# Second attention layer: six more source tiles as two float32r parts, with their 0/1 matrices cast on GpSimd

## The chip, the core and the metric

The kernel runs on one core of a Trainium2 chip, in one launch. Engines are called by the profile's names: PE is TensorE's matmul, PEld its weight load, DVE is VectorE, ACT is ScalarE, POOL is GpSimd, SP is the engine that issues most DMAs. The metric is device time in microseconds (us), the median of the runs shown. Before the change it is 3557.16 us, with runs of 3549.43, 3557.16 and 3558.97.

## The reference

Four graph layers follow each other on x (3327 nodes, 512 features) with one adjacency matrix. Each adds its result to x after a layer norm and a relu. Layers 0 to 2 are attention layers with 8, 4 and 8 heads, layer 3 averages neighbours. The change is in layer 1, the second one:

```python
def _L1_gnn_ref(H, A, W, a_l, a_r):
    mask = A + jnp.eye(n, dtype=A.dtype) > 0
    Wh = (H @ W).reshape(n, N_HEADS, D_K)              # 4 heads of 128
    sl = jnp.einsum('nhd,hd->nh', Wh, a_l)
    sr = jnp.einsum('nhd,hd->nh', Wh, a_r)
    e = jax.nn.leaky_relu(sl[:, :, None] + sr.T[None, :, :], negative_slope=NEG_SLOPE)
    e = jnp.where(mask[:, None, :], e, -jnp.inf)
    alpha = jnp.nan_to_num(jax.nn.softmax(e, axis=2), nan=0.0)
    out = jnp.einsum('nhm,mhd->nhd', alpha, Wh).reshape(n, OUT_DIM)
    return jax.nn.elu(out)
```

## The kernel before, in words

Nodes are cut into 26 tiles of 128. Query tiles are worked on in seven chunks, six of four tiles and a last one of two. Source tiles lie in five groups, `JG`: three of six tiles (g0, g1, g2) and two of four (g3, g4).

The exponential of a leaky relu of a sum splits into a product of a query factor and a source factor, one such product (a = 0) where the sum is positive and another (a = 1) where it is not. So a head needs two matrix products: a 0/1 matrix that says which edges lie on the positive side, times a table of source rows scaled by the first factor; and the matrix of the remaining edges, times a table scaled by the second. Each table has 128 features and one column for the softmax's denominator, 129 columns in all.

For one head of one chunk, `attention` does this in layer 1. `matrices` makes the 0/1 matrices: a compare for each source tile (L670 on ACT, or L667 on DVE for tiles 18 to 25), then an AND with the mask (L674, DVE). They are fp8, in tiles called `tht`. After the products of a = 0 an exclusive or with the mask (L794, DVE) turns the same tile into the matrix of a = 1. The products run in passes: a pass is two query tiles against all 26 source tiles, so 52 matmuls, and a full chunk has 4 heads x 2 products x 2 passes = 16 passes. The layer has 104 passes, eight of them in the last chunk. A pass ends with two reductions on DVE that add the parts and leave PSUM (L780).

The table rows are float32 and are kept to float32's precision in one of two ways, by the group's letter in `KIND = "bssvv"`:

- "b" (g0): three bf16 pieces side by side, 387 columns. The fp8 matrix is the stationary operand as it is (L762).
- "s" (g1, g2) and "v" (g3, g4): two float32r parts, 258 columns (L759). The matrix is first copied to float32r by `real` (L639): on ACT into `ts` (three buffers) for "s", on DVE into `tv` (two buffers) for "v". One copy serves one pass.

The tables are loaded from HBM by SP for each head and each a (L714), one DMA a group, into a ring of seven equal buffers `ab`. They are written in the layer before by `pieces` (three bf16 pieces, with subtractions on POOL) or by `parts` (a copy on ACT and a subtraction on DVE).

Work for the next layer is strewn between the passes by `hooks.run`: for each finished query tile an elu and an add (L866 to L869, the add on POOL), a layer norm (the small POOL steps L350 to L352), a projection on PE (L413), the scaling of its tables (L450, DVE) and their three pieces (L387 on DVE, L391 and L397 on ACT, L395 on POOL).

Tiles come from pools with a fixed number of buffers, and a planner writes the final order of each engine's instructions, ahead of the program's order where buffers allow it. On the engine the order is then fixed: an instruction that waits holds up all behind it on that engine.

Of the kernel before, what the change touches and what calls it, by code (L numbers as in the profile page):

```python
# [25 lines left out]
F32 = mybir.dt.float32  # L26
BF16 = mybir.dt.bfloat16
# [10 lines left out]
P = 128  # L38
# [7 lines left out]
GP_ON_DVE = [(5, 12, 19), tuple(range(18, 26)), (4, 9, 14, 19, 24)]  # L46


KIND = "bssvv"


@with_exitstack
def tile_gnn(ctx: ExitStack, tc: tile.TileContext, x, adj, W0, a01, W1, al, ar, W2, a2,
# [60 lines left out]
    for l in range(3):  # L114
        H, DA, AO, HW = dims(l)
        if l == 1:
            abd.append([dram.tile([H, 2, P, nj, AO], BF16, name=f"ab{l}_{g}") if KIND[g] == "b" else
                        dram.tile([H, 2, P, nj, 2 * DA], F32, name=f"ab{l}_{g}") for g, (_, nj) in enumerate(JG)])
        else:
            abd.append([dram.tile([H, P, nj, HW], BF16, name=f"ab{l}_{g}") for g, (_, nj) in enumerate(JG)])  # L120
    y1d = [dram.tile([n * P, D], F32, name=f"y1_{c}") for c, (_, n) in enumerate(chunks)]
# [247 lines left out]
    def pieces(L, t, AB, pool, first, behind=None):  # L369

        l = L.l
        g, jj = jwhere[t]
        H, DA, AO, HW = dims(l)

        o, two = (t % 2, 2) if first else (0, 1)
        if o == 0:
            L.pt = pool.tile([P, H, 2, two, AO] if l == 1 else [P, H, two, HW], BF16, name="pt", bufs=3 if first else 2)
        pt = L.pt
        nc.gpsimd.memset(pt[:, :, :, o, 3 * DA:AO] if l == 1 else
                         pt[:, :, o].rearrange("p h (a w) -> p h a w", a=2)[..., 3 * DA:AO], 1.0)  # L380

        def dst(s, a):
            if l == 1:
                return pt[:, :, a, o, s * DA:(s + 1) * DA]
            return pt[:, :, o, a * AO + s * DA:a * AO + (s + 1) * DA]
        r = pool.tile([P, 2, H, DA], F32, name="r", bufs=2 if first else 1)
        sb = nc.vector.tensor_sub(r, AB, high(AB))  # L387
        if behind:
            after(sb, behind)
        for a in range(2):  # L390
            cp = nc.scalar.copy(dst(0, a), high(AB[:, a]))  # L391
            if behind:
                after(cp, behind)
        for a in range(2):
            nc.gpsimd.tensor_sub(dst(2, a), r[:, a], high(r[:, a]))  # L395
# [3 lines left out]
        if o == two - 1 and l == 1:  # L399
            for a in range(2):  # L400
                L.to_store.append((abd[l][g][:, a, :, js, :].rearrange("h p j w -> p h j w"), pt[:, :, a]))
        elif first and o == two - 1:
# [52 lines left out]
    def parts(L, t, AB, pool, first, behind=None):  # L455
# [2 lines left out]
        g, jj = jwhere[t]  # L458
        H, DA, AO, HW = dims(l)
        H2 = H // 2  # L460
        if l == 1 and KIND[g] != "b":
            for f in range(2):
                hs = slice(f * H2, (f + 1) * H2)
                pt = pool.tile([P, H2, 2, 2, DA], F32R, name="pt", bufs=2)
                v = pt.rearrange("p h a s d -> p s a h d")
                cp = nc.scalar.copy(v[:, 0], AB[:, :, hs])
                if behind:
                    after(cp, behind)
                nc.vector.tensor_sub(v[:, 1], AB[:, :, hs], v[:, 0].bitcast(F32))
# [164 lines left out]
    def real(a, g, ks, th):  # L634

        nj = JG[g][1]
        k0, k1 = ks[0], ks[-1] + 1
        t = mp.tile([P, 2, nj, P], F32R, name="ts" if KIND[g] == "s" else "tv", bufs=3 if KIND[g] == "s" else 2)
        (nc.scalar.copy if KIND[g] == "s" else nc.vector.tensor_copy)(t[:, :k1 - k0, :nj], th[a][g][:, k0:k1])  # L639
        return t  # L640

    ahead = {}
# [42 lines left out]
    def attention(L, hooks, open_next, close):  # L685
# [5 lines left out]
        for c, (t0, nt) in enumerate(chunks):  # L691
# [3 lines left out]
            for h in range(H):  # L695
# [47 lines left out]
                for a in range(2 if l == 1 else 1):  # L743
# [5 lines left out]
                    for ks, js in passes:  # L749
                        thr = {}  # L750
                        for j in js:
                            g, jj = jwhere[j]
                            if l == 1 and KIND[g] != "b" and g not in thr:
                                thr[g] = real(a, g, ks, th)
                            for k in ks:
                                if j == 0:
                                    acc[k] = accs.tile([P, 512], F32, name="acc")
                                if g in thr:
                                    mm = nc.tensor.matmul(acc[k][:, :2 * DA], thr[g][:, k - ks[0], jj, :], ab[a][g][:, jj, :],  # L759
                                                     start=(j == 0), stop=(j == NT - 1), skip_group_check=True)  # L760
                                elif l == 1:
                                    mm = nc.tensor.matmul(acc[k][:, :3 * DA], th[a][g][:, k, jj, :], ab[a][g][:, jj, :3 * DA],  # L762
                                                     start=(j == 0), stop=(j == NT - 1), skip_group_check=True)
                                else:
                                    o = 1 if deg else 0
# [11 lines left out]
                            continue  # L777
                        for k in ks:
                            if l == 1:
                                nc.vector.tensor_reduce(R[:, k, a, :], acc[k][:, :3 * DA].rearrange("p (s d) -> p d s", s=3),  # L780
                                                        AX.X, ALU.add)
                            else:
                                v = acc[k][:, :2 * AO].rearrange("p (a w) -> p a w", a=2)[:, :, :3 * DA]
# [114 lines left out]
    with tc.tile_pool(name="first", bufs=1) as fp:  # L898
# [47 lines left out]
        while hooks.small:  # L946
# [1 line left out]
    A, R = [("A", D, F32, n) for n in A_BUFS], ("R", PER * 2 * 129, F32, 1)  # L948
    ab, gt, tht = ("ab", JM * 400, BF16, 7), ("gt", PER * JM * P, FP8, 7), ("tht", PER * JM * P, FP8, 7)
    tags = [[A[0], ("R", PER * 2 * 65, F32, 1), tht, ("tr", JM * P, BF16, 5), ("abx", 4 * 400, BF16, 4), gt],  # L950
            [A[1], ("ab", JM * 258, F32R, 7), R, ("ts", 2 * JM * P, F32R, 3), ("tv", 2 * 4 * P, F32R, 2), tht[:3] + (10,)],
            [A[2], ab, ("R", PER * 2 * 65, F32, 1), tht, gt]]
    hooks.masks = in_steps([mask_steps(ip, t, g) for t, g in order[20:]])
    for l in range(3):
# [530 lines left out]
```

## Time and profile before

| what | value |
| --- | --- |
| median of three runs | 3557.16 us |
| the profiled execution's span | 3551.1 us |
| PE, PEld busy | 3442.3 us (97%), 3107.2 us (88%) |
| DVE, ACT, POOL busy | 2624.3 us (74%), 2507.0 us (71%), 618.8 us (17%) |
| layer 1's passes | from 1233 to 2072 us of the span |
| in there: PE, DVE, ACT, POOL busy | 822.8, 729.3, 705.4, 205.5 of 839 us |
| in there: DMA | 78% of the DMA engines' time, 279 GB/s |

The page gives no time for the profiled execution beside its span. The span lies between the fastest and the slowest of the three runs.

Busy time of an engine is the union of its instructions' spans. A row of the order of time gives start, duration, engine, line, operation and tiles, and in brackets how long the engine had idled before and what ended that. A row by shape gives the count, the busy time, the mean duration of one, and the idle time before. In a row of windows each engine has its busy time and its number of instructions, then come the granted clock of PE, the DMA share and GB/s.

### The profile page before, as it was taken

What the parts mean: (1) busy time and instruction counts of PE and PEld (TensorE: products, weight loads), DVE (VectorE), ACT (ScalarE), POOL (GpSimd) and SP (SyncE); (2) the same over time, 40 slices, a digit from 0 to 9 for tenths busy, and PEclk for the clock granted to TensorE, in tenths of its full rate; (3) what the DMA queues carried; (4) which work ended last, traced back from release to release, by engine and by line L of the source; (5) the groups of instructions that cost most, each with busy time, mean ns of one, the idle gap of its engine ahead of it and who ended that gap; (6) DMA issues with size and microseconds to landing.
All of it is one profiled execution on the core that took longest, in us unless ns stands there. A gap on an engine that the chain in (4) does not pass through costs nothing. (4 is left out here: it accounts for less than half of the span.)

```text
span 3551.1 us, 77646 instructions
## 1 busy us (share of the span) xinstructions
PE 3442.3 (97%) x30751; PEld 3107.2 (88%) x30751; DVE 2624.3 (74%) x5227; ACT 2507.0 (71%) x4113; POOL 618.8 (17%) x858
## 2 busy tenths in 40 slices
PE   7899999999999999999999989999999999999998
PEld 6789999999999888888888869989898989876887
DVE  7788888888887699888888868867676768672121
ACT  5777787878787789888888677767666757572111
POOL 6611222112111202222223320101010101020000
PEclk9999999999999999999999999999999999999999
DMA  7699999999857787777777875555545555576331
GB/s 207 223 282 251 233 263 238 268 260 250 256 203 247 246 285 276 279 269 273 269 273 254 332 268 190 191 175 189 183 166 181 185 172 188 168 271 257 105 107 54
DMA packets 398120, 797.72 MB, mean 225 GB/s; under 512 B 112970, under 2 KB 221845, under 8 KB 397105
## 3 DMA queue, kind: packets, MB, share of 16 engines
q1 hardware_dynamic: 363890, 723.14, 63.4%
q0 software_dynamic: 28128, 62.42, 7.6%
q10 hardware_dynamic: 5726, 7.08, 0.6%
q8 instruction: 245, 4.01, 0.5%
q14 instruction: 131, 1.07, 0.1%
HBM read 663.59 MB, written 129.64 MB: 223 GB/s over the span
## 5 line engine op out<-in xcount | busy, mean ns | idle before, releaser
L670 ACT ACTIVATE gt<-s1b,ks 128x512 fp8e4<-128x512 f32 (+1 forms) x2448 | 1448.2, 677 | 276.4 <-issue 160.1
L766 PE MATMUL acc<-ab,tht 128*128 128x195 bf16 (+1 forms) x9112 | 1553.1, 248 | 5.4 <-DVE tht L674 4.6
L769 PE MATMUL acc<-ab,gt 128*128 128x195 bf16 (+1 forms) x9112 | 1552.2, 248 | 5.0 <-DVE rc L806 3.3
L769 PEld LDWEIGHTS <-gt 128*128 128x128 fp8e4 x10744 | 1053.6, 98 | 40.1 <-issue 27.4
L766 PEld LDWEIGHTS <-tht 128*128 128x128 fp8e4 x10744 | 1053.4, 98 | 24.8 <-DVE tht L674 11.5
L674 DVE TENSOR_TENSOR tht<-gt,m 128x768 uint32<-128x768 uint32 (+3 forms) x557 | 445.5, 800 | 129.4 <-ACT gt L670 125.5
L676 DVE TENSOR_TENSOR gt<-tht,m 128x768 uint32<-128x768 uint32 (+3 forms) x557 | 448.0, 805 | 8.7
L639 ACT CAST ts<-tht 128x1536 fp32r<-128x1536 fp8e4 x208 | 300.0, 1470 | 55.6 <-PE acc L759 52.5
L759 PE MATMUL acc<-ab,ts 128*128 128x258 f32 x2496 | 333.4, 289 | 4.7 <-ACT ts L639 3.4
L759 PEld LDWEIGHTS acc<-ab,ts 128*128 128x128 f32 x2496 | 313.2, 190 | 13.2 <-ACT ts L639 3.8
L667 DVE TENSOR_SCALAR gt<-s1b,ns 128x512 fp8e4<-128x512 f32 (+1 forms) x446 | 218.2, 495 | 129.4 <-PE acc L769 125.1
L1021 PE MATMUL acc<-y,mf 128*128 128x512 f32 x1352 | 309.8, 391 | 1.1 <-DVE mf L1016 1.1
L670 ACT ACTIVATE tht<-s1b,ks 128x512 fp8e4<-128x512 f32 (+1 forms) x504 | 308.4, 680 | 2.3 <-DMA s1b<-s 1.7
L1021 PEld LDWEIGHTS acc<-y,mf 128*128 128x128 f32 x1352 | 253.6, 188 | 57.2 <-DVE mf L1016 1.5
L769 PE MATMUL acc<-abx,gt 128*128 128x195 bf16 (+1 forms) x1632 | 287.4, 249 | 11.6 <-DVE rc L806 5.6
L766 PE MATMUL acc<-abx,tht 128*128 128x195 bf16 (+1 forms) x1632 | 287.8, 249 | 4.6 <-DVE tht L674 3.0
L869 POOL TENSOR_TENSOR xt<-xt,e 128x512 f32<-128x512 f32 x72 | 121.9, 1693 | 916.8 <-DVE e L868 583.9
L784 DVE TENSOR_REDUCE R<-acc 128x130 f32<-128x390 f32 x416 | 214.2, 554 | 79.5 <-PE acc L769 78.9
L762 PE MATMUL acc<-ab,tht 128*128 128x387 bf16 x1248 | 225.8, 329 | 8.9 <-DMA ab<-ab 5.8
L1018 ACT CAST mf<-m 128x768 fp32r<-128x768 fp8e4 (+1 forms) x78 | 59.1, 762 | 244.5 <-PE acc L1021 232.7
L759 PE MATMUL acc<-ab,tv 128*128 128x258 f32 x1664 | 218.8, 283 | 1.4 <-DVE tv L639 1.2
L759 PEld LDWEIGHTS acc<-ab,tv 128*128 128x128 f32 x1664 | 207.2, 189 | 2.9 <-DVE tv L639 2.1
(163 smaller groups left out, 3710.2 us busy)
## 6 DMA issues: line engine op xcount, KB each, us to landing
ab<-ab SPq DMA_DIRECT2D x333, 600.0 KB, 5.3
ab<-ab SPq DMA_DIRECT2D x112, 774.0 KB, 6.5
ab<-ab SPq DMA_DIRECT2D x112, 516.0 KB, 5.3
ab<-ab SPq DMA_DIRECT2D x112, 400.0 KB, 4.0
abx<-ab SPq DMA_DIRECT2D x110, 400.0 KB, 7.9
ab<-ab SPq DMA_DIRECT2D x56, 582.0 KB, 7.3
s1b<-s SPq DMA_DIRECT2D x120, 256.0 KB, 6.5
m<-mask SPq DMA_DIRECT2D x69, 384.0 KB, 4.4
```

What stands on the lines that cost most here:

```text
L639: (nc.scalar.copy if KIND[g] == "s" else nc.vector.tensor_copy)(t[:, :k1 - k0, :nj], th[a][g][:, k0:k1])
L667: nc.vector.tensor_scalar(gv[:, :, jj, :], s1v, L.ns2[:, j, h:h + 1], 2.0, op0=ALU.is_gt, op1=ALU.mult, saturate=False)
L670: nc.scalar.activation(gv[:, :, jj, :], s1v, AF.Relu, bias=L.ks2[:, j, h:h + 1], scale=BIG, saturate=False)
L674: nc.vector.tensor_tensor(pu, gu, mu, ALU.bitwise_and)
L676: nc.vector.tensor_tensor(gu, pu, mu, ALU.bitwise_xor)
L759: mm = nc.tensor.matmul(acc[k][:, :2 * DA], thr[g][:, k - ks[0], jj, :], ab[a][g][:, jj, :], start=(j == 0), stop=(j == NT - 1), skip_grou ...
L762: mm = nc.tensor.matmul(acc[k][:, :3 * DA], th[a][g][:, k, jj, :], ab[a][g][:, jj, :3 * DA], start=(j == 0), stop=(j == NT - 1), skip_grou ...
L766: nc.tensor.matmul(acc[k][:, :3 * DA + o], th[0][g][:, k, jj, :], ab[0][g][:, jj, :3 * DA + o], start=(j == 0), stop=False, skip_group_che ...
L769: mm = nc.tensor.matmul(acc[k][:, AO:AO + 3 * DA + o], th[1][g][:, k, jj, :], ab[0][g][:, jj, AO:AO + 3 * DA + o], start=False, stop=(j == ...
L784: nc.vector.tensor_reduce(R[:, k], v.rearrange("p a (s d) -> p a d s", s=3), AX.X, ALU.add)
L869: nc.gpsimd.tensor_add(xt, xt, e)
L1021: nc.tensor.matmul(acc[k], mf[:, jj, :], y2[g][:, jj, s, :], start=(j0 + jj == 0 and s == 0), stop=(j0 + jj == NT - 1 and s == 1))
```

## The change

`KIND` becomes "gssvv". g0 is now treated as g1 to g4 are: two float32r parts, 258 columns, one matmul form for the whole layer. Its 0/1 matrix is copied from fp8 to float32r on POOL, 128x1536 elements a pass, into a new tile `tg` with two buffers. The bf16 pieces of layer 1 disappear, with their storage in HBM. The reduction at the end of a pass reads 258 columns instead of 387. Buffers change: the ring of seven `ab` becomes a ring of four for the groups of six tiles and a ring of three for the groups of four, and `tht` has nine buffers instead of ten.

```diff
-KIND = "bssvv"
+KIND = "gssvv"
...
         if l == 1:
-            abd.append([dram.tile([H, 2, P, nj, AO], BF16, name=f"ab{l}_{g}") if KIND[g] == "b" else
-                        dram.tile([H, 2, P, nj, 2 * DA], F32, name=f"ab{l}_{g}") for g, (_, nj) in enumerate(JG)])
+            abd.append([dram.tile([H, 2, P, nj, 2 * DA], F32, name=f"ab{l}_{g}") for g, (_, nj) in enumerate(JG)])
...
-        if l == 1 and KIND[g] != "b":
+        if l == 1:
             for f in range(2):
...
-        t = mp.tile([P, 2, nj, P], F32R, name="ts" if KIND[g] == "s" else "tv", bufs=3 if KIND[g] == "s" else 2)
-        (nc.scalar.copy if KIND[g] == "s" else nc.vector.tensor_copy)(t[:, :k1 - k0, :nj], th[a][g][:, k0:k1])
+        copy = {"g": nc.gpsimd.tensor_copy, "s": nc.scalar.copy, "v": nc.vector.tensor_copy}[KIND[g]]
+        t = mp.tile([P, 2, nj, P], F32R, name="t" + KIND[g], bufs=3 if KIND[g] == "s" else 2)
+        copy(t[:, :k1 - k0, :nj], th[a][g][:, k0:k1])
...
-                            tl = mp.tile([P, JM * 2 * DA], F32R, name="ab", bufs=7)
-                            two = KIND[g] != "b"
-                            w = 2 * DA if two else AO
-                            v = (tl if two else tl.bitcast(BF16))[:, :nj * w].rearrange("p (j w) -> p j w", j=nj)
-                            ld = nc.sync.dma_start(v.bitcast(F32) if two else v, abd[l][g][h, a])
+                            v = mp.tile([P, nj, 2 * DA], F32R, name=f"ab{nj}", bufs=4 if nj == JM else 3)
+                            ld = nc.sync.dma_start(v.bitcast(F32), abd[l][g][h, a])
...
-                        pt = mp.tile([P, PER * JM * P], FP8, name="tht", bufs=10 if l == 1 else 7)
+                        pt = mp.tile([P, PER * JM * P], FP8, name="tht", bufs=9 if l == 1 else 7)
...
-                            if l == 1 and KIND[g] != "b" and g not in thr:
+                            if l == 1 and g not in thr:
                                 thr[g] = real(a, g, ks, th)
...
-                                elif l == 1:
-                                    mm = nc.tensor.matmul(acc[k][:, :3 * DA], th[a][g][:, k, jj, :], ab[a][g][:, jj, :3 * DA],
-                                                     start=(j == 0), stop=(j == NT - 1), skip_group_check=True)
...
-                                nc.vector.tensor_reduce(R[:, k, a, :], acc[k][:, :3 * DA].rearrange("p (s d) -> p d s", s=3),
+                                nc.vector.tensor_reduce(R[:, k, a, :], acc[k][:, :2 * DA].rearrange("p (s d) -> p d s", s=2),
                                                         AX.X, ALU.add)
```

More of the change, by code (lines that the diff above doesn't have):

```diff
@@ L376, in pieces @@
         if o == 0:
-            L.pt = pool.tile([P, H, 2, two, AO] if l == 1 else [P, H, two, HW], BF16, name="pt", bufs=3 if first else 2)
+            L.pt = pool.tile([P, H, two, HW], BF16, name="pt", bufs=3 if first else 2)
         pt = L.pt
-        nc.gpsimd.memset(pt[:, :, :, o, 3 * DA:AO] if l == 1 else
-                         pt[:, :, o].rearrange("p h (a w) -> p h a w", a=2)[..., 3 * DA:AO], 1.0)
+        nc.gpsimd.memset(pt[:, :, o].rearrange("p h (a w) -> p h a w", a=2)[..., 3 * DA:AO], 1.0)
         def dst(s, a):
-            if l == 1:
-                return pt[:, :, a, o, s * DA:(s + 1) * DA]
             return pt[:, :, o, a * AO + s * DA:a * AO + (s + 1) * DA]
@@ L398, in pieces @@
         js = slice(jj + 1 - two, jj + 1)
[L399 to L402, printed above, removed]
+        if first and o == two - 1:
             if g not in ahead:
@@ L950, in tile_gnn @@
     tags = [[A[0], ("R", PER * 2 * 65, F32, 1), tht, ("tr", JM * P, BF16, 5), ("abx", 4 * 400, BF16, 4), gt],
-            [A[1], ("ab", JM * 258, F32R, 7), R, ("ts", 2 * JM * P, F32R, 3), ("tv", 2 * 4 * P, F32R, 2), tht[:3] + (10,)],
+            [A[1], ("ab6", JM * 258, F32R, 4), ("ab4", 4 * 258, F32R, 3), R, ("ts", 2 * JM * P, F32R, 3),
+             ("tg", 2 * JM * P, F32R, 2), ("tv", 2 * 4 * P, F32R, 2), tht[:3] + (9,)],
             [A[2], ab, ("R", PER * 2 * 65, F32, 1), tht, gt]]
```

## The prediction

> **What bounds the kernel now.** I read the page's busy shares, then windows over layer 1, then the order of time inside a pass, then rows by shape, and last POOL's rows. The windows (us; PE, PEld, DVE, ACT, POOL busy; clock, DMA share, GB/s), the second and third one full chunk each:
>
> ```profile
> 1300.00:1400.00 100.00, 98.30 (x744) 86.59 (x743) 95.06 (x177) 84.82 (x104) 13.99 (x14) 1.00 0.77 283
> 1493.70:1618.90 125.20, 125.01 (x915) 109.99 (x914) 110.23 (x203) 108.80 (x146) 32.77 (x37) 1.00 0.78 273
> 1618.90:1744.20 125.30, 125.29 (x918) 110.34 (x918) 109.72 (x201) 108.85 (x146) 35.65 (x38) 1.00 0.78 274
> 2000.00:2072.00 72.00, 61.21 (x391) 51.66 (x392) 50.92 (x114) 42.70 (x74) 26.93 (x37) 0.95 0.92 346
> ```
>
> In a steady chunk PE never stops, at full clock; DVE and ACT are 88% and 87% busy. In the last chunk PE loses some 11 of 72 us, with the DMA engines at 92%. So PE's own work sets the time in six chunks of seven, and DVE is next in line. A pass in the order of time:
>
> ```profile
> 1600.57 2.15 PE L762 MATMUL acc<-ab,tht 128*128 128x387 bf16 x12
> 1602.42 3.19 PE L759 MATMUL acc<-ab,ts 128*128 128x258 f32 x24
> 1605.44 2.08 PE L759 MATMUL acc<-ab,tv 128*128 128x258 f32 x16
> 1607.36 2.15 PE L762 MATMUL acc<-ab,tht 128*128 128x387 bf16 x12
> ```
>
> The starts give 1.85 us for g0's 12 matmuls (154 ns each), 3.02 us for 24 in float32r (126 ns), 6.79 us for the pass.
>
> How POOL and DVE get on decides the rest. The rows of the order of time, first one in which POOL waits, then one in which DVE does:
>
> ```profile
> 1618.76 2.15 DVE L794 TENSOR_TENSOR tht<-tht,m 128x768 uint32<-128x768 uint32 x3
> 1618.92 4.59 POOL L869 TENSOR_TENSOR xt<-xt,e 128x512 f32<-128x512 f32 x1 [0.70 <-DVE e L868]
> 1620.84 0.94 DVE L674 TENSOR_TENSOR tht<-tht,m 128x768 uint32<-128x768 uint32 x1
> 1621.71 0.68 DVE L639 CAST tv<-tht 128x1024 fp32r<-128x1024 fp8e4 x1
> 1622.31 1.01 DVE L780 TENSOR_REDUCE R<-acc 128x129 f32<-128x387 f32 x2
> 1623.55 0.63 ACT L866 ACTIVATE e<-A 128x512 f32<-128x512 f32 x1 [4.22 <-POOL xt L869]
> ```
>
> ```profile
> 1608.63 2.51 POOL L395 TENSOR_TENSOR pt<-r 128x520 bf16<-128x520 f32 x2 [15.94 <-DVE r L387]
> 1610.15 2.08 DVE L802 TENSOR_TENSOR R<-R,cpm 128x1032 f32<-128x1032 f32 x1
> ```
>
> The add L869 takes 1.26 us alone and 4.59 here: it gets in only when DVE reaches L780, which reads PSUM. The multiply L802, 1.22 us alone (at 1795.51), takes 2.08 behind L395. DVE work from SBUF and POOL work exclude each other; only DVE's idle time and its PSUM readers are free for POOL.
>
> **The change, part by part.**
>
> PE. Per pass 12 matmuls go from 154 to 126 ns: 0.34 us, 5.4 us per full chunk (125.2 to 119.8), 32.6 us for the 96 passes of full chunks, 35.4 for all 104.
>
> DVE. L780 takes 550 ns for 387 columns. L804 shows the price of a column: 287 ns for 130 elements and 420 for 260, 1.02 ns each. 129 columns fewer are 0.13 us, 32 reductions a chunk give 4.3 us. DVE goes from 110.0 (mean of the two full chunks) to 105.7 before the casts.
>
> The cast on POOL: 104 times 128x1536, fp8 to float32r, one input. No row has it. POOL's one-input rows:
>
> ```profile
> 1.18 0.28 POOL masks.py:199 TENSOR_SCALAR_AFFINE_SELECT ident<-ident 128x128 f32<-128x128 f32 x1
> L283 POOL COPY m<-dg x26: 199/209/1183, 1107.4 to 1972.2; 128x32 uint32<-128x32 uint32 x26
> L350 POOL TENSOR_SCALAR mv<-mv x104: 216/422/1111, 5.1 to 3213.2; 128x1 f32<-128x1 f32 x104
> L395 POOL TENSOR_TENSOR pt<-r x116: 1043/1057/4064, 31.4 to 2105.0; 128x520 bf16<-128x520 f32 x104, 128x516 bf16<-128x516 f32 x12
> ```
>
> (In the last three, the least, median and greatest ns.) From 216 ns for one element to 284 for 128 is 0.5 ns an element, 1.0 us for the cast: the lower end. From the 32-element copy (199) to 284 is 0.88: 199 + 1504 x 0.88 = 1.5 us. Two-input rows give 2.0 (L395) to 2.46 (L869) ns an element: 3.1 to 3.8 us, the upper end. I take 1.5, from the two one-input rows nearest to it, and keep 1.0 to 3.8. [...]
>
> What a cast costs DVE. Per chunk DVE leaves POOL 15.2 idle + 16.3 (L780, half of its 32.6 in the two chunks) + 5.1 (L450) = 36.6 us. POOL now has 8 subtractions of 1.05 and 4 adds of 1.26 a chunk, 13.4 us; DVE's instructions of the two chunks, each against the lowest tenth of its shape, are 14.3 us longer, 7.1 a chunk: 53%. For 16 x 1.5 = 24 us that is 12.7. Laying one cast per pass into the first free stretch after its buffer is released, on DVE's order of time of four chunks, leaves 10.1 us blocked. DVE then has 105.7 + 10.1 to 12.7 = 115.8 to 118.4 of 119.8 us, 97 to 99%. [...]
>
> What PE loses at such a load: in 1300 to 1400 DVE was 95% busy and PE 98.3% (the row above), 1.7%. I take 2% of six chunks (719 us), 14 us; between 0 and the whole 32.6.
>
> What queues behind the cast on POOL: adds, norm steps, subtractions, and the stores that POOL issues. ACT already waited 4.22 us for an add; a cast in front adds up to 1.5 us to some of 24. This is in the 2%. The casts themselves are early in the built order: 88 of 104 can start 91 or more of the layer's matmuls before the first that needs them, 11 us, and the laying above never takes longer than 10.4. Two have no lead, at the layer's start and in the last head's first pass. At the first, PE waits for the cast too: 1.5 us (0 to 3). At the other PE already waited 3.4 us for ACT's copy in the same place: 1 us (0 to 3).
>
> Loads. g0 grows from 582 to 774 KB, 56 times; SP now issues g3's load ahead of g1's, since its ring is its own. In full chunks the rings tell more: release to use shrinks from 61 to 65 matmuls to 53 for three of five groups, 8.4 to 6.5 us, against 6.5 us median from issue to landing of a 774 KB load and 5.3 of a 516 KB one. So no cover is left. At 0 to 0.8 us in each of 48 table rows this is 0 to 38 us; I take it as hidden in the 14 us, because a pass that waits for DVE gives a load the same time. In the last chunk 8 x 192 KB more at 346 GB/s are 4.5 us, and its 2.7 us of saved matmuls are lost to the DMA: 2 us taken (-2.7 to 4.5).
>
> `tht` with nine buffers: the tenth matrix now waits for g0's release, which the last cast gives nearly a pass before the last matmul did. PE waits 2.7 us for such matrices in the layer now; I take 0, between -2.7 and as much again. In layer 0 six tiles lose POOL subtractions (2.4 us a tile), four ACT copies become two, and one DVE subtraction of 1.23 us becomes two of 0.69: 0.9 us more on DVE in all, hidden under PE, which the page shows at 9 tenths there; 0, at most 0.9.
>
> Sum: -32.6 + 14 + 1.5 + 1 + 2 = -14 us. The profiled span of 3551 becomes 3537; from the median 3557 it is 3543.
>
> **Rivals.**
>
> Slow cast (ends slower). A cast of 2.6 us, between the one- and two-input rows, laid in the same way blocks 26 us a chunk: DVE 131.7 against 125.2 before, 6.5 x 6 = +39 and the edges: 3600. It decides at about 2.2 us, where DVE reaches 125. At 3.1 us it is +80. [...] Against: affine select.
>
> Waits eat it. The cast has 1.5 us, but at 97 to 99% DVE is late often enough to use up all of PE's gain: 3557 (3547 to 3570). For it: in-order queues and two-deep rings. Against: DVE waited 55 us for `tv` buffers alone, so it runs ahead.
>
> Late loads. 0.5 us in 48 rows on top of the rest: 3543 + 24 = 3567. For it: no cover. Against: three loads a row are issued 12 matmuls apart and need not queue.
>
> All of it comes. DVE stays ahead as at 88%: 3557 - 35 + 5 = 3527.
>
> **How the numbers follow.** Chances: forecast 0.47, slow cast 0.23, waits eat it 0.16, late loads 0.07, all of it 0.07. 0.3% is 10.7 us, about what a measurement tells from no change. The forecast's own range, 3531 to 3553, lies for seven tenths below 3546: faster 0.33 + 0.07 + 0.01 = 0.41. Same: 0.12 of the forecast, 0.08 of the waits, 0.01: 0.21. Slower 0.38. The range goes from the whole gain, 3527, to a cast of 2.8 us, 3612.
>
> **What would show it.** L759 with `tg` at about 126 ns a matmul and a pass of 6.45 us. The cast's least duration 1.5 us, its mean above 2. DVE above 95% in a chunk, with L639, L667, L802 and L809 longer. A chunk of 121 to 123 us. Wrong, if the cast takes 2.2 us or more alone, if PE idles before `tg` matmuls in steady chunks, or if DMA ends PE's waits there.

## The result, and the profile after

The change makes the kernel slower. The kernel after takes 3602.47 us (median of four runs, 3599.09 to 3604.38), the kernel before beside it 3553.30 (3548.75 to 3558.97). The ratio is 1.0138, with a 95% interval of 1.0123 to 1.0152. The forecast was 3543 us, a gain of 14; the outcome is a loss of 49. It lies inside the range, on the other side of the time before.

The page of the kernel after begins with the busy shares of its span of 3597.3 us:

```profile
PE 3427.8 (95%) x30751; PEld 3163.8 (88%) x30751; DVE 2693.7 (75%) x5233; ACT 2500.6 (70%) x4101; POOL 781.9 (22%) x944
```

PE's work is down by 14.5 us, DVE's is up by 69 and POOL's by 163. Over the whole span no share looks alarming, so the stage has to be read. Its windows, with the columns of the prediction's windows (us; PE, PEld, DVE, ACT, POOL busy; clock, DMA share, GB/s), are cut where every 832nd matmul of the layer begins; 832 matmuls are one full chunk. The first row is the second chunk, the last row the short last one:

```profile
1360.70:1495.60 134.90, 123.19 (x912) 118.62 (x913) 127.81 (x212) 110.67 (x149) 58.09 (x50) 0.96 0.73 258
1495.60:1625.70 130.10, 119.39 (x915) 115.05 (x914) 124.73 (x204) 117.01 (x160) 61.49 (x53) 1.00 0.77 279
1625.70:1759.50 133.80, 121.29 (x916) 116.46 (x914) 125.99 (x203) 110.45 (x147) 57.21 (x53) 0.99 0.75 270
1759.50:1891.90 132.40, 122.28 (x916) 117.98 (x915) 123.24 (x201) 109.21 (x145) 61.15 (x53) 0.97 0.76 269
1891.90:2024.90 133.00, 123.20 (x915) 119.41 (x914) 121.31 (x211) 104.76 (x150) 57.04 (x51) 0.96 0.74 260
2024.90:2115.00 90.10, 75.82 (x501) 70.67 (x500) 70.04 (x143) 56.33 (x98) 46.69 (x48) 0.91 0.93 348
```

Where the clock is 1.00 PE's work of a chunk is 119.39 us: the cheaper matmuls did come, 119.8 was forecast. But a chunk takes 130 to 135 us where it took 125. PE now idles some 11 us in it, and DVE is busy for 121 to 128 us, longer than PE's work. Cut in the same way, the traces of before and after give:

| layer 1, us | before | after |
| --- | --- | --- |
| first chunk | 124.1 | 127.4 |
| mean of chunks 2 to 6 | 125.7 | 132.9 |
| last chunk | 86.6 | 90.2 |
| all passes | 839.1 | 881.9 |
| PE idle in them | 15.9 | 80.3 |

So 43 of the 46 us between the two spans lie in layer 1, and 36 of them in five steady chunks.

The cast itself, from the answer on tile `tg` (least, median and greatest ns, first and last start in us):

```profile
L633 POOL CAST tg<-tht x104: 1458/1481/5020, 1227.6 to 2098.2; 128x1536 fp32r<-128x1536 fp8e4 x104
```

1.46 us alone; 1.5 was forecast. What it does to DVE is seen in the rows by shape of the layer (count, busy us and mean ns, idle us before). First before, then after:

```profile
L639 DVE CAST tv<-tht 128x1024 fp32r<-128x1024 fp8e4 x208 | 145.9, 702 | 55.1 <-PE acc L759 55.1
L667 DVE TENSOR_SCALAR tht<-s1b,ns 128x512 fp8e4<-128x512 f32 x192 | 93.8, 536 | 0.9 <-PE acc L762 0.9
L674 DVE TENSOR_TENSOR tht<-tht,m 128x768 uint32<-128x768 uint32 x72 | 67.9, 950 | 7.0 <-ACT tht L670 6.9
```

```profile
L633 DVE CAST tv<-tht 128x1024 fp32r<-128x1024 fp8e4 x208 | 168.0, 810 | 24.2 <-PE acc L750 24.2
L661 DVE TENSOR_SCALAR tht<-s1b,ns 128x512 fp8e4<-128x512 f32 x192 | 127.1, 701 | 0.0
L668 DVE TENSOR_TENSOR tht<-tht,m 128x768 uint32<-128x768 uint32 x71 | 78.2, 1101 | 11.8 <-ACT tht L664 11.5
```

The same instructions on the same shapes are 108, 165 and 151 ns longer in the mean. The reductions L768, which read PSUM, are not: all 208 took 405 to 430 ns. DVE's slack is seen in the idle time before `tv`: it waited 55.1 us for PE to free these buffers, and now 24.2. To put one number on it I take, for every DVE instruction of the layer, its duration less the lowest tenth of its operation and shape, and call the sum DVE's lengthening. It is 7.5 us in a steady chunk before and 24.8 after: 17.3 more for 16 casts, 1.08 us for each cast of 1.48. (Against the kernel without the cast, below, it is 15.2 us, 0.95 for each.)

One such place in the order of time (start, duration; in brackets the idle time before):

```profile
1643.16 1.92 DVE L661 TENSOR_SCALAR tht<-s1b,ns 128x512 fp8e4<-128x512 f32 x1
1643.30 1.48 POOL L633 CAST tg<-tht 128x1536 fp32r<-128x1536 fp8e4 x1
1644.99 0.68 DVE L633 CAST tv<-tht 128x1024 fp32r<-128x1024 fp8e4 x1
1645.59 0.47 DVE L661 TENSOR_SCALAR tht<-s1b,ns 128x512 fp8e4<-128x512 f32 x1
1645.73 1.22 PE L750 MATMUL acc<-ab,tv 128*128 128x258 f32 x8
1647.26 0.67 DVE L633 CAST tv<-tht 128x1024 fp32r<-128x1024 fp8e4 x1
1647.99 1.23 PE L750 MATMUL acc<-ab,tv 128*128 128x258 f32 x8 [1.04 <-DVE tv L633]
```

The compare L661 takes 0.47 us when nothing stands in its way (1645.59) and 1.92 when the cast runs inside it (1643.16): the difference, 1.45 us, is nearly the whole cast of 1.48. The two `tv` casts behind it come late, and PE stands still for 1.04 us before the second. The waits of the stage, by engine, line and cause (us in total, times, longest):

```profile
POOL tg L633 <- PE acc L750: 167.0, 38, 12.9
PE acc L750 <- DVE tv L633: 29.1, 23, 2.9
PE acc L750 <- DMA ab<-ab: 25.0, 22, 3.4
ACT e L854 <- POOL xt L857: 23.0, 9, 6.1
PE acc L750 <- ACT ts L633: 8.6, 7, 2.9
```

In the kernel before, the waits for tables, for `tv` and for the add were:

```profile
PE acc L762 <- DMA ab<-ab: 5.8, 3, 3.0
PE acc L759 <- DMA ab<-ab: 1.2, 2, 1.0
PE acc L759 <- DVE tv L639: 1.2, 2, 0.7
ACT e L866 <- POOL xt L869: 25.2, 10, 5.2
```

PE waits for DVE's copies first, and nearly as long for tables from HBM. POOL itself waits 167 us for PE to free `tg`, so it isn't short of time. But its cast comes too late in places, for DVE and not for PE: the exclusive or L782 overwrites a matrix that the cast must have read, and waits for it.

```profile
DVE tht L782 <- POOL tg L633: 14.6, 7, 2.6
```

### The profile page after: what moved, and what is told of

Its sections match the earlier page's. It is cut to its first block, busy times and chain, and to the rows that moved or that the text cites. A ratio compares the mean times of both kernels' runs of the same rounds, so it can differ in the third digit from the quotient of the medians.

```text
span 3597.3 us, 77815 instructions
## 1 busy us (share of the span) xinstructions
PE 3427.8 (95%) x30751; PEld 3163.8 (88%) x30751; DVE 2693.7 (75%) x5233; ACT 2500.6 (70%) x4101; POOL 781.9 (22%) x944
## 5 line engine op out<-in xcount | busy, mean ns | idle before, releaser
L757 PEld LDWEIGHTS <-gt 128*128 128x128 fp8e4 x10744 | 1053.3, 98 | 35.3 <-issue 24.8
L661 DVE TENSOR_SCALAR gt<-s1b,ns 128x512 fp8e4<-128x512 f32 (+1 forms) x446 | 217.1, 492 | 137.5 <-PE acc L757 133.4
L664 ACT ACTIVATE tht<-s1b,ks 128x512 fp8e4<-128x512 f32 (+1 forms) x504 | 309.6, 679 | 10.4 <-DMA s1b<-s 10.1
L750 PE MATMUL acc<-ab,tv 128*128 128x258 f32 x1664 | 229.5, 288 | 35.3 <-DVE tv L633 29.1
L633 POOL CAST tg<-tht 128x1536 fp32r<-128x1536 fp8e4 x104 | 181.3, 1747 | 239.8 <-PE acc L750 167.0
```

What stands on the lines that cost most here:

```text
L633: copy(t[:, :k1 - k0, :nj], th[a][g][:, k0:k1])
L661: nc.vector.tensor_scalar(gv[:, :, jj, :], s1v, L.ns2[:, j, h:h + 1], 2.0, op0=ALU.is_gt, op1=ALU.mult, saturate=False)
L664: nc.scalar.activation(gv[:, :, jj, :], s1v, AF.Relu, bias=L.ks2[:, j, h:h + 1], scale=BIG, saturate=False)
L757: mm = nc.tensor.matmul(acc[k][:, AO:AO + 3 * DA + o], th[1][g][:, k, jj, :], ab[0][g][:, jj, AO:AO + 3 * DA + o], start=False, stop=(j == ...
```

## The experiments

Three theories stood against each other, and the recorded expectations use their letters. P: POOL's cast and DVE's work in SBUF exclude each other, DVE falls behind PE, and PE waits for `tv`. L: the loads are late, because g0's tables are larger and the ring of seven buffers became rings of four and three. Q: POOL's queue is the trouble, since adds and stores wait behind casts. Each median below stands beside runs of the kernel before on the same chip, whose median was 3553 to 3557 us. "The passes" are the time from layer 1's first matmul of the passes to the end of the last.

**No cast at all.** One constant tile of ones takes the place of g0's matrix. This leaves out g0's proper contribution to the products.

```diff
         copy = {"g": nc.gpsimd.tensor_copy, "s": nc.scalar.copy, "v": nc.vector.tensor_copy}[KIND[g]]
+        if KIND[g] == "g":
+            if not fixed:
+                fixed.append(mp.tile([P, 2, nj, P], F32R, name="tg", bufs=1))
+                nc.vector.memset(fixed[0].bitcast(F32), 1.0)
+            return fixed[0]
```

> The changed kernel with GpSimd's cast left out: the matmuls of the first six source tiles read one constant float32r matrix instead, so those tiles' contribution to the second layer is left out of the result in its proper form. Matmuls, loads, buffer rings and all other work stay. [...] Theory L (the smaller rings of four and three make the table loads late): the loads still come late, 3570 to 3595 us. [...]

3534.82 us, ratio 0.9938 (0.9920 to 0.9957). The cast costs 67.7 us, 0.65 for each. The spans of the two traces differ by 63 us: 51 of them lie in the layer's passes, which take 831.0 us here, and 8 ahead of the passes, where neither kernel casts. By P and by Q the loss had to go with the cast, by L not, so the time alone doesn't tell P from Q. Two chunks of this kernel, with the columns as above:

```profile
1477.30:1599.80 122.50, 118.62 (x916) 114.96 (x915) 111.50 (x205) 116.15 (x159) 33.63 (x37) 1.00 0.82 293
1599.80:1722.40 122.60, 119.15 (x915) 115.95 (x914) 110.79 (x207) 110.98 (x151) 30.10 (x37) 0.99 0.83 293
```

DVE falls from some 125 us a chunk to 111, and PE's waits for `tv` from 29.1 us to under 1. What is left of PE's waits is L:

```profile
PE acc L756 <- DMA ab<-ab: 26.5, 24, 4.4
```

**No cast, and one ring of seven for all tables.** The same constant tile, and:

```diff
-                            v = mp.tile([P, nj, 2 * DA], F32R, name=f"ab{nj}", bufs=4 if nj == JM else 3)
+                            tl = mp.tile([P, JM * 2 * DA], F32R, name="ab", bufs=7)
+                            v = tl[:, :nj * 2 * DA].rearrange("p (j w) -> p j w", j=nj)
```

> As the kernel without the cast (the same part is left out), and the rings of four and three table buffers are one ring of seven again. Theory P: within 5 us of the kernel without the cast. Theory L: 15 to 40 us less than that one, and PE's waits for table loads, 25 us in the changed kernel's second layer, fall below 10 us.

3521.15 us, ratio 0.9903 (0.9882 to 0.9924): 13.7 us less than with the split rings; the passes alone take 808.9 us, 22 less. Neither expectation is met: P had at most 5 us, L at least 15 and waits below 10. PE's waits for tables are halved:

```profile
PE acc L757 <- DMA ab<-ab: 12.7, 11, 5.2
```

So L is real and worth 14 us where nothing else holds PE up, a fifth of the cast's price (22 of 51 in the passes alone). This kernel also shows that PE's gain is there for the taking: 33 us below the 3553.89 of before beside it, where 35.4 us of matmul time go.

**The cast made twice.**

```diff
         copy(t[:, :k1 - k0, :nj], th[a][g][:, k0:k1])
+        if KIND[g] == "g":
+            copy(t[:, :k1 - k0, :nj], th[a][g][:, k0:k1])
```

> The changed kernel with every cast made twice into the same tile: 104 more casts of 1.47 us, 153 us of GpSimd work. Theory P: VectorE is blocked for about eight tenths of it more and is already what PE waits for, so 100 to 150 us more than the changed kernel, 3700 to 3750. Theory L: no more than 20 us more, 3602 to 3622. Theory Q: between, 3620 to 3680, with ScalarE's waits for GpSimd twice as long.

3714.43 us, ratio 1.0438 (1.0410 to 1.0467). The second cast costs 112 us, 1.08 for each, as P expected and neither L nor Q. In steady chunks DVE's lengthening goes from 24.8 to 41.6 us, 1.05 us per added cast; DVE and the clock are seen in the windows of two of them:

```profile
1538.90:1689.80 150.90, 129.15 (x915) 124.41 (x914) 141.66 (x203) 110.08 (x145) 89.14 (x69) 0.92 0.66 234
1689.80:1836.20 146.40, 126.98 (x916) 122.22 (x915) 139.23 (x202) 109.63 (x146) 90.06 (x69) 0.93 0.68 244
```

The lengthening per cast is about that of the first, but the time per cast is 1.08 and no longer 0.65: I read this as slack that the first cast used up (DVE's, and PE's waits for tables) and the second no longer found. POOL is still at 60% of the chunk.

**The cast in two halves** of 128x768, in case a long instruction shuts DVE out longer than it must.

```diff
+        if KIND[g] == "g":
+            for k in range(k1 - k0):
+                copy(t[:, k, :nj], th[a][g][:, k0 + k])
+        else:
+            copy(t[:, :k1 - k0, :nj], th[a][g][:, k0:k1])
```

> The changed kernel with every cast made in two instructions, one for each query tile: 128x768 elements each, by the least durations of before and after about 0.8 us. [...] If what counts is GpSimd's busy time alone: 104 more starts of some 0.2 us, 3602 to 3625. Theory L: 3600 to 3605.

3607.31 us, ratio 1.0147 (1.0123 to 1.0171): no different from the whole cast. If a long instruction shut DVE out longer than it must, the halves would have gained; the time fits POOL's busy time alone. The halves take 814 ns at least, so two take 1.63 us against 1.46; the lengthening stays at 24.5 us a chunk.

**A write without a read.** POOL fills `tg` with ones at the place of the cast. g0's proper contribution is again left out.

```diff
+        if KIND[g] == "g":
+            nc.gpsimd.memset(t[:, :k1 - k0, :nj].bitcast(F32), 1.0)
+        else:
+            copy(t[:, :k1 - k0, :nj], th[a][g][:, k0:k1])
```

> The changed kernel with a GpSimd memset of the same 128x1536 float32r tile in the place of the cast: it writes, but reads nothing, so the first six source tiles get a constant 0/1 matrix and their proper contribution is left out. By the memset rows of before (204 ns for 128 elements, 544 for 512) it takes about 1.4 us, nearly as long as the cast, stands in the same queue and uses the same two buffers; only the wait for the 0/1 matrix is gone. Theory Q (GpSimd's queue is what is late): as the changed kernel, 3590 to 3605 us. Theory P, all of VectorE's work from SBUF excluded: the same, 3585 to 3605. Theory P with the read side alone counting for two-input work: VectorE's ANDs and exclusive ors stay at their lengths and only its copies and compares are blocked, 3545 to 3580.

3574.54 us, ratio 1.0055 (1.0036 to 1.0074), 28 us less than with the cast. This lies in the range of P with two-input work spared, and 15 us below Q's. The fill takes 1373 ns at least, so POOL's queue is nearly as long as with the cast. By shape:

```profile
L636 DVE CAST tv<-tht 128x1024 fp32r<-128x1024 fp8e4 x208 | 180.6, 871 | 22.8 <-PE acc L753 22.8
L664 DVE TENSOR_SCALAR tht<-s1b,ns 128x512 fp8e4<-128x512 f32 x192 | 115.1, 639 | 3.3 <-ACT ts L636 3.3
L671 DVE TENSOR_TENSOR tht<-tht,m 128x768 uint32<-128x768 uint32 x72 | 72.5, 1007 | 12.4 <-ACT tht L667 12.3
```

DVE's one-input work is longer beside the fill as beside the cast: the copies take 871 ns (810 with the cast, 737 with neither), the compares 639 (701 and 517). The two-input AND is not: 1007 ns, where it takes 1002 in the kernel without any cast and 1101 with it. Here, then, a write alone lengthened DVE's copies and compares, and the AND only got longer where POOL reads too. How the 28 us divide stays open: DVE's lengthening is 22.9 us a chunk, little less than the 24.8 with the cast, but the fill is also 0.1 us shorter, waits for no matrix, and DVE's exclusive or needn't wait for it (14.6 us with the cast).

**The cast on DVE.**

```diff
-        copy = {"g": nc.gpsimd.tensor_copy, "s": nc.scalar.copy, "v": nc.vector.tensor_copy}[KIND[g]]
+        copy = {"g": nc.vector.tensor_copy, "s": nc.scalar.copy, "v": nc.vector.tensor_copy}[KIND[g]]
```

> The changed kernel with the cast on VectorE instead of GpSimd, 104 times 128x1536. From the 128x1024 cast's 0.68 us it takes 0.95 to 1.0 us, about 100 us of VectorE in all, where the GpSimd cast lengthened VectorE's work by some 19 us a full chunk, 120 us in all. Theory P: about level with the changed kernel or a little faster, 3575 to 3600. Theory Q: GpSimd's queue is free again, 3540 to 3565.

3563.56 us, ratio 1.0027 (1.0013 to 1.0042), 39 us faster than with the cast on POOL. This is outside P's 3575 to 3600 and inside Q's 3540 to 3565. Alone it would speak for Q. Against Q stand the fill, which holds POOL's queue for nearly as long as the cast, and ACT's waits for the add, which did not grow with the casts on POOL (23.0 us, 25.2 before).

Against the kernel without the cast, the cast costs 29 us on DVE (0.28 for each) and 68 on POOL (0.65). DVE, nominally the busier engine, does it more cheaply itself. Yet the two load DVE nearly alike, as the means of five steady chunks show:

| g0's cast, us a chunk | chunk | PE idle | DVE busy | DVE's lengthening |
| --- | --- | --- | --- | --- |
| none | 123.8 | 4.6 | 110.5 | 9.6 |
| on DVE | 125.2 | 5.6 | 121.9 | 10.1 |
| fill on POOL | 128.5 | 8.2 | 120.9 | 22.9 |
| on POOL | 132.9 | 11.0 | 124.6 | 24.8 |

With the fill DVE is a little less busy than with its own cast, and the chunk is 3.3 us longer. What PE loses thus doesn't follow from DVE's load alone. POOL's work may hit DVE just when a copy for PE is next, while DVE's own cast has its place in DVE's order; no run here tests that.

**The kernel before, with the cast thrown in.** A cast of g0's matrix per pass into a tile that nobody reads, so PE needs nothing of it. `tht` gives up its tenth buffer for room.

```diff
+                            if l == 1 and j == 0:
+                                tg = mp.tile([P, 2, JM, P], F32R, name="tg", bufs=1)
+                                nc.gpsimd.tensor_copy(tg[:, :len(ks), :], th[a][0][:, ks[0]:ks[-1] + 1])
```

> The kernel before, its three bf16 pieces and its ring of seven kept, with the same GpSimd cast once a pass into a tile that nobody reads, and nine buffers for the 0/1 matrices instead of ten. PE needs nothing of the cast. Theory P: VectorE had 15 us to spare in a full chunk of 125 and gets 12 to 19 us longer, so it turns late in places: 3565 to 3605 us. Theory L (rings) and the theory that it is the matrices' path over GpSimd that is late: no difference, 3550 to 3562.

3659.24 us, ratio 1.0297 (1.0279 to 1.0314). Its control is **the kernel before with nine `tht` buffers** and nothing else:

```diff
-                        pt = mp.tile([P, PER * JM * P], FP8, name="tht", bufs=10 if l == 1 else 7)
+                        pt = mp.tile([P, PER * JM * P], FP8, name="tht", bufs=9 if l == 1 else 7)
```

> The kernel before with nine tht buffers instead of ten, nothing else: a control for the kernel before with the cast thrown in, which had to give up that buffer too. If the buffer matters little, 3550 to 3562; if it explains a part of that kernel's +104 us, more than 3570.

3565.21 us, ratio 1.0033 (1.0020 to 1.0046): the buffer costs 12 us there, the cast alone 94. A steady chunk, first with the cast and then in the control:

```profile
1512.30:1655.50 143.20, 131.97 (x916) 114.65 (x915) 128.65 (x203) 108.98 (x146) 63.82 (x53) 0.95 0.69 238
```

```profile
1616.20:1742.90 126.70, 125.27 (x915) 109.97 (x913) 112.79 (x203) 107.87 (x146) 31.26 (x37) 1.00 0.76 269
```

16.4 us longer in the mean of five chunks, 1.03 us per cast, and 16.7 us more of lengthening on DVE. No matmul waits for `tg` here and the loads are those of before, so P needs neither L nor a wait for the cast. What PE waits for is `tv`, 59.6 us (2.1 in the control). The outcome lies far above P's 3565 to 3605, and L's "no difference" is out; the control lies between its two expectations.

**The casts dealt over three engines.** Of eight passes three cast on DVE, three on POOL, two on ACT.

```diff
+        who = nc.gpsimd.tensor_copy
+        if KIND[g] == "g":
+            who = (nc.vector.tensor_copy, nc.gpsimd.tensor_copy, nc.scalar.copy)[(0, 1, 2, 0, 1, 2, 0, 1)[len(turns) % 8]]
+            turns.append(g)
```

> The changed kernel with the casts dealt out over the engines, in every eight passes three on VectorE, three on GpSimd, two on ScalarE. A full chunk then has six casts of 0.95 us on VectorE, six of 1.47 on GpSimd that block it for some 0.65 to 1.1 us each, and four of 1.47 us on ScalarE, whose load goes from 109 to 115 us. Theory P: VectorE at 116 to 118 us, less than the 124 of the changed kernel: 3550 to 3585 us. Theory Q: 3550 to 3570.

3560.16 us, ratio 1.0009 (0.9998 to 1.0021): level with before, and inside both P's and Q's ranges. DVE's lengthening is 14.4 us a chunk.

**One ring of seven with the cast on each engine.** The ring as above; to make room `tg` has one buffer. First with the cast on DVE, then dealt out, then on POOL:

```diff
-        t = mp.tile([P, 2, nj, P], F32R, name="t" + KIND[g], bufs=3 if KIND[g] == "s" else 2)
+        t = mp.tile([P, 2, nj, P], F32R, name="t" + KIND[g], bufs={"g": 1, "s": 3, "v": 2}[KIND[g]])
```

> g0's cast on DVE instead of POOL, one ring of seven buffers for all tables, one tg buffer. Theory P (POOL's cast and DVE's SBUF work exclude each other): with the cast on DVE alone the lengthening is gone (the same kernel with the rings of four and three took 3563.6 us); what is left is the ring, which was worth 13.7 us where there was no cast. So 3550, between 3543 and 3560, waits of PE for tables 12 to 16 us. If the ring gives less, because DVE is now nearly as busy as PE and late anyway: 3560 to 3566. Tells whether the two causes add.

> The casts dealt out (of eight: three on DVE, three on POOL, two on ACT) with one ring of seven. The same dealing with rings of four and three took 3560.2 us. If the ring is worth 10 to 14 us here too: 3546 to 3550, a little faster than before; the gain of PE's matmuls (35 us) then is paid back by engines that are late by turns. If the one tg buffer costs what the ring gives: 3560.

> The change as it is, but one ring of seven and one tg buffer. If the loads were the main loss: about 3550. If POOL's cast against DVE is: 3580 to 3600, with PE's waits for tables down by 8 to 12 us and its waits for tv not lower.

3566.92 us (1.0038, 1.0024 to 1.0052), 3571.67 (1.0045, 1.0030 to 1.0061) and 3594.95 (1.0113, 1.0098 to 1.0127). The ring with one `tg` buffer gives 7.5 us with the cast on POOL, nothing on DVE, and with the dealt casts it costs 12. In all three PE's waits for tables fall (to 5.5, 8.4 and 6.8 us), and other waits take their place: for `tv` on POOL's variant (40.1 us, 29.1 before the ring), for `tg` on DVE's (16.7, 10.5 before). I had expected the ring's 14 us to add up (3543 to 3560 on DVE, or up to 3566 with DVE late anyway; 3546 to 3550 dealt out, or else 3560; 3580 to 3600 on POOL, the only range met). They don't; but the second `tg` buffer went with the ring, so a late engine and the lost buffer aren't told apart.

**Eleven `tht` buffers**, paid for with the second `tg` buffer, since the control had shown a price for the tenth. Cast on POOL, on DVE, and by turns on DVE and ACT:

```diff
-                        pt = mp.tile([P, PER * JM * P], FP8, name="tht", bufs=9 if l == 1 else 7)
+                        pt = mp.tile([P, PER * JM * P], FP8, name="tht", bufs=11 if l == 1 else 7)
```

> The change with eleven tht buffers instead of nine, paid for with the second tg buffer; cast on POOL, rings of four and three. In the kernel before, ten to nine buffers cost 12 us. If that is a cost of its own, apart from POOL against DVE: 3585 to 3592. If it is hidden behind the late DVE here, as the ring mostly was: 3595 to 3605. In both cases PE's waits for tv stay above 25 us.

> Cast on DVE, one tg buffer, eleven tht buffers, rings of four and three. With nine and two tg buffers it took 3563.6 us. If the tht buffers' 12 us come back: 3548 to 3556, about level with before. If not: 3560 to 3567.

> Casts by turns on DVE and ACT, none on POOL, one tg buffer, eleven tht buffers. DVE has some 50 casts of 1.0 us fewer than with all on it, ACT some 50 more. If engine load and the buffers are the whole of what is left: 3540 to 3550, faster than before. If a cast that waits on its one buffer in ACT's or DVE's queue holds up the ones behind it: 3560 or more.

3602.03 us (1.0138, 1.0123 to 1.0152), 3565.51 (1.0028, 1.0017 to 1.0040), 3559.73 (1.0014, 1.0002 to 1.0026). On POOL and on DVE this changes nothing, and the third is not the 3540 to 3550 that buffers alone would have given. The two edits go together, so it isn't shown that the ninth buffer is free in the changed kernel, only that two more are not worth more than one `tg` buffer.

**By turns on DVE and ACT, with the change's own buffers.**

```diff
+        who = nc.gpsimd.tensor_copy
+        if KIND[g] == "g":
+            who = (nc.vector.tensor_copy, nc.scalar.copy)[len(turns) % 2]
+            turns.append(g)
```

> Casts by turns on DVE and ACT with the change's own buffers (two tg, nine tht, rings of four and three). Dealt over three engines it took 3560.2 us. Without POOL's share DVE's lengthening goes from 85 back to about 58 us: 3550 to 3558. If ACT's share costs as much as POOL's: 3560 to 3570. Beside the run with eleven and one it tells what the buffers are worth when POOL has no part.

3548.93 us, ratio 0.9984 (0.9974 to 0.9994). It is the only full kernel below the one before, by 0.16%, less than the 0.3% that the prediction named as measurable; I call it level, though the passes of its trace, 828.1 us, are 11 us shorter than before. It is just below the 3550 to 3558 expected. Two chunks and the last one:

```profile
1481.30:1601.80 120.50, 117.94 (x916) 114.68 (x915) 114.77 (x211) 114.94 (x147) 32.77 (x37) 1.00 0.83 294
1601.80:1723.70 121.90, 117.94 (x915) 114.69 (x914) 114.34 (x209) 118.31 (x154) 37.99 (x37) 1.00 0.84 294
1971.70:2065.90 94.20, 74.80 (x500) 69.38 (x499) 68.44 (x151) 62.83 (x108) 35.20 (x41) 0.91 0.91 332
```

With DVE near 115 us and ACT near 117 a chunk takes 121.9 us in the mean, 3.8 less than before. But the last chunk is 8 us longer than before (94.4 and 86.6), with the DMA engines at 91%, which gives back two fifths of the 19 us that five chunks gain. With one `tg` and eleven `tht` the same casts took 11 us more (3559.73), so the second `tg` buffer is worth more than two of `tht`.

## Why the prediction was wrong

The direction failed at one place, the load on DVE and what PE loses by it. The fourth step below rests on one row of PE's order of time in the kernel before:

```profile
1303.13 2.48 PE L762 MATMUL acc<-ab,tht 128*128 128x387 bf16 x14 [1.70 <-DMA ab<-ab]
```

By the prediction's own steps:

- **PE.** "5.4 us per full chunk (125.2 to 119.8)" held: 119.39 us of work at full clock.
- **The cast on POOL.** "I take 1.5" held: 1.46 to 1.48 us. The reading from affine select and the 32-element copy was right, and the "slow cast" did not happen. That rival's 3600 us is near the outcome for another reason, so it is luck that the range, whose upper part was laid out for it, holds the outcome.
- **What a cast costs DVE.** This is the first step that failed. "12.7" by the share of 53%, and "10.1 us blocked" by laying casts into free stretches, measured 17.3 us a chunk against the kernel before and 15.2 against the one without the cast. The share was 64 to 73% of the casts' time, and the laying had let every cast wait for a stretch that suits it, where on the chip a cast starts when its matrix and its buffer are there: 38 of the 104 start the moment PE frees `tg`, whatever DVE is doing then. That this is why the laying failed is argued, not shown. The base failed too: "105.7 before the casts" is 110.5 us in the kernel without the cast. The reductions did get shorter (416 ns for 550), but DVE's other instructions there are 2.1 us a chunk longer, and a few more of them fall in these chunks (1035 in five, 1012 before). With the casts the windows show 124.6 us in the mean of five. "115.8 to 118.4 of 119.8" was thus 6 to 9 us short, and on the wrong side of PE's 119.8.
- **What PE loses at such a load.** "I take 2% of six chunks (719 us), 14 us; between 0 and the whole 32.6." This is the term that turned the sign. The six chunks went from 752.5 to 791.6 us, +39.1, where the gain was -32.6: PE lost 72 us, a tenth, of which the split rings have a part. The 2% was misread. The 1.7 us that PE idled from 1300 to 1400 are one wait, and it is for a table, not for DVE. So that stretch shows no loss to DVE at a load of 95%, and no price for a higher one. With the casts DVE is busy 124.6 us a chunk, 4.8 more than PE's 119.8, but the chunk is 13 longer; waits for tables are 3.9 of that. The thrown-in cast, with the loads of before, shows the same: DVE is busy 128.4 us in a chunk of 143.2, where PE's work took 125.3. So PE loses more than DVE's excess. The runs show that POOL's casts cause it; why it is so much larger than the excess stays open. And the bound "the whole 32.6" was no bound, since a DVE that needs longer than PE can cost more than the change gains. The cast thrown into the old kernel shows it without any gain: +94 us.
- **Loads.** "I take it as hidden in the 14 us, because a pass that waits for DVE gives a load the same time." Measured, PE waits 25.0 us for tables in the changed kernel (7.0 before) and 26.5 without the cast, where DVE waits are gone. The first half failed: they aren't hidden. The second was half right: the ring that was worth 13.7 us alone is worth 7.5 where DVE is late, with one `tg` buffer less.
- **`tht` with nine buffers.** "I take 0, between -2.7 and as much again." In the kernel before it costs 12 us; in the changed kernel no cost of its own could be shown.
- **Queue behind the cast.** ACT's waits for the add are 23.0 us in 9 waits (25.2 in 10 before), and none of PE's larger waits ends there. PE's wait for `tg` itself is 2.9 us, with 2.5 taken. By the adds Q is not the cause. That a waiting instruction holds up those behind it does show in the trace of before: behind the add that ACT waited 4.22 us for, a `ts` copy started at 1624.08, though PE had last raised the semaphore it waits for at 1621.17. Not in the sum was DVE's wait of 14.6 us until the cast has read its matrix; the thrown-in cast costs 94 us without it.
- **Layer 0, last chunk.** The first matmul of the layer's passes starts at 1233.3 us in both traces. That is one trace each: over all kernels here it starts between 1225.2 and 1246.4 us, so a cost of 0.9 can't be told. The last chunk is 3.6 us longer, 2 was taken. These terms are too small to matter.
- **What the prediction had no step for.** Where PE's gaps were long (2.4 and 3.4 us in one chunk) its clock fell, to 0.96 in that chunk, and the work itself got longer, see below: 3.8 us, 123.20 for 119.39. Over the layer's passes the mean clock goes from 0.99 to 0.97. PE's idle time there grows by 64 us, and its work falls by 22 where 35 was forecast.
- **The signs.** "Its mean above 2" was 1.75 us: a cast loses 0.3 us in the mean, where DVE loses about 1. "A chunk of 121 to 123 us" was 132.9. Of the three signs of being wrong one came plainly: in the five steady chunks DMA ends 19.4 us of PE's waits. PE's largest wait there, 23.8 us for `tv`, was not among the signs.

By the medians, the loss of 49 us is made up of a gain of 32.7 (the kernel without the cast and with one ring, of the 35.4 forecast), less 13.7 for the split rings (measured without the cast), less 67.7 for the cast (measured with the split rings). In the traces of the layer's passes alone the three are 30.2, 22.1 and 50.9, a loss of 42.8; the cast is the larger cost either way, but the sizes differ by 8 and 17 us between the two reckonings. The two costs hide part of each other, so the split depends on the order in which they are taken away.

## What to carry to other kernels

An engine with idle time is not free if its work makes that of the engine next in line longer: price an instruction on POOL by the time that it takes from DVE, here 0.95 to 1.08 us for a cast of 1.48, which DVE does by itself in 0.95; and it can cost the kernel more than that work done on DVE (0.65 us a cast against 0.28 here). A loss read from a busy stretch is a price of that load only if the wait in it ends there. When the new load of the second engine lands within a few per cent of the bound, there is no upper limit at "the gain is lost"; work out what happens if it passes the bound, and give that its chance. And a buffer edit that comes along (a split ring, one buffer fewer) should be priced alone, though its price may vanish behind a later engine.

## What the runs showed of the hardware

**PE's clock fell after a step of 3.41 us in which PE had idled 1.88 us or more.** Of the changed kernel's chunks the one from 1495.6 us has 10.7 us of idle PE, no gap over 1.6 us, clock 1.00 and 119.39 us of work. The one from 1891.9 has less idle, 9.8 us, but gaps of 2.4, 3.4 and 1.9 us; its clock is 0.96 and the same work takes 123.20. The windows around the first two, which end at 1914.2 and 1929.0 us:

```profile
1910.00:1920.00 10.00, 7.62 (x51) 7.42 (x50) 10.00 (x15) 4.40 (x6) 7.47 (x8) 0.83 0.27 107
1920.00:1930.00 10.00, 6.52 (x47) 5.99 (x46) 9.46 (x14) 9.73 (x14) 3.50 (x4) 0.95 0.83 273
1930.00:1940.00 10.00, 10.00 (x63) 9.48 (x62) 9.32 (x21) 7.78 (x11) 2.81 (x4) 0.88 0.37 150
1940.00:1950.00 10.00, 10.00 (x83) 9.88 (x83) 10.00 (x19) 9.85 (x15) 4.13 (x2) 1.00 0.79 269
```

In the ten microseconds after the second gap PE is busy all the time, but at a granted clock of 0.88: 1.2 us of ten are lost on top of the gap. The record of the granted clock in the traces of before and after changes only at multiples of a step of 3.41 us, between 1.00 and 0.50. In layer 1's passes of the two traces, 14 steps at 1.00 had PE idle for 1.88 us, somewhat more than half of a step, or longer, and each was followed by a step at 0.50; the other 467, with 1.76 us at most, never were. So it counts where a gap falls: gaps of 2.9 and 3.0 us that began at 1442.9 and 1466.6 us in the changed kernel fell across two steps, with at most 1.66 us in each, and left the clock at 1.00.

**Casting in halves didn't let DVE in.** Two POOL casts of 0.81 us lengthened DVE's work by as much as one of 1.46 (24.5 and 24.8 us a chunk).

**A write alone lengthened DVE's one-input work.** The fill that reads nothing left the copies at 871 ns and the compares at 639, against 737 and 517 in the kernel without a cast. The AND stayed at 1007 ns against 1002, so the prediction's "DVE work from SBUF and POOL work exclude each other" is too wide for this pair.
